# Four image layers on one core: layer 1's buffers placed over those its neighbours release first, with its norm's sums and its attention turns rearranged

## The chip, the cores and the metric

The kernel runs on one core of a Trainium2 chip. A core has a matrix engine (TensorE, called PE; its weight loads are listed apart as PEld), a vector engine (VectorE, DVE), a scalar engine (ScalarE, ACT) and a general one (GpSimd, POOL), and a sequencer that only issues transfers (SyncE, SP). ACT and POOL can issue transfers too, each on a queue of its own. Each engine works through its instructions in order and waits for others by semaphores. The metric is the time of one execution on the device in microseconds (us). Three runs of the kernel before took 5497.55, 5501.04 and 5502.83 us.

## What is computed

Eight images of 56 x 56 points and 192 channels pass four layers. Each layer adds its result to its input, and its input is first normalized over groups of channels (`_gn`). Cut to what matters here:

```python
# layer 0: gated Toeplitz products along rows and columns
p, q, v = silu(x @ p_w.T + p_b), silu(x @ q_w.T + q_b), silu(x @ v_w.T + v_b)
out = (p * (toeplitz_rows(q * v, a1) + toeplitz_cols(q * v, a2))) @ o_w.T + o_b
# layer 1: layer norm over channels, roll by (3, 3), attention in 7 x 7 windows
x = (x - mu) * rsqrt(var + EPS) * gamma + beta
win = roll(x, (-3, -3)) cut into 64 windows of 49 points
attn = softmax(q * scale @ k.T + rel_bias + mask)      # 6 heads of 32
out = roll((attn @ v) @ w_proj + b_proj, (3, 3))
# layer 2: projection to 384 channels, 3 x 3 convolution, four scans, norm, projection back
proj = einsum('bhwd,dc->bhwc', x, W_in) + b_in
local = conv3x3(proj)
mixed = 0.25 * (scan_lr + scan_rl + scan_tb + scan_bt) + local
out = layernorm(mixed) @ W_out + b_out
# layer 3: 7 x 7 convolution, layer norm, two dense layers with gelu
x = x + L0(_gn(x)); x = x + L1(_gn(x)); x = x + L2(_gn(x)); x = x + L3(_gn(x))
```

## The kernel before

The four layers run one after the other, each for all eight images. Between layers the images go through DRAM: layer 0 writes `x1`, layer 1 writes `x2`, the first half of layer 2 writes `pd`. A layer's buffers come from pools that are opened for it and closed after it, so a new pool lies over the memory of an old one. A tile's first write then waits until all that lay there has been read, tile by tile. Layer 0's and layer 1's image buffers stand at the right end of the memory (`raws`, then `l1x` with three buffers), the others at the left, in the order in which they are first asked for.

**Layer 0** ends, for each image, with gates: `layer0_gate` (L475) goes over four pieces of 392 columns and for each projects, applies silu, turns the Toeplitz result and multiplies, and adds the output to the image; `layer0_gate_last` (L539) does so for the last 64 channels. Beside image b+1's products run the store of image b to `x1` and the statistics of image b (`stats`, L610: 12 `bn_stats` on DVE and an aggregate). For the last image these come after everything else (L696 to L699). The Toeplitz results stand in two buffers `os`; the last channels' results share the first of them.

**Layer 1** works on an image in four groups of 16 windows. `layer1_norm` (L775) is a generator: a plan of letters decides when each of its steps is issued. It copies the image, scaled by the group norm, into windows (`windows`, eight copies for a group, into `xr`), squares them on ACT (`squares`), sums channels of the windows and of their squares with matmuls against `ones32` (L844 and L848: for two groups, three channel blocks each, 12 matmul calls), forms the variance (L855, L859), then `rs = (var + eps) ** -0.5` by three small steps (`finish`: DVE, ACT logarithm L820, ACT exponential L822), spreads it over the partitions with a matmul (L827, `rstd`) and multiplies the windows by it on DVE (L832, `scaled`). For image 0 (`first`) the copies are shared by POOL, ACT and DVE, and the sums come for group 0, group 1, and groups 2 and 3.

`layer1_scores` (L873) projects queries and keys (letter Q, L886), values (V, L901) and the scores (E, L916). On DVE the bias and mask are added (L921) and the maximum taken (L923), POOL subtracts it (L924); in the next group ACT takes the exponential (X, L928), DVE sums (L933) and inverts (L934), POOL multiplies (Y, L935). `layer1_mix` (L942) turns the shares with PE transposes (T, L956, three tiles `et_ps` for each half image), copies them out (L961 on ACT, L963 on DVE), multiplies them with the values (P, L971, two tiles `po`), and projects (R, L990 and L997; added to the image by DVE at L1004). PE's results stand in PSUM in rings of buffers: three named "mm" (projections, values, sums, `rstd`, the first half of `pr`, and the third turn), two named "et" (the first and second turn, `po`, the second half of `pr`).

The order in layer 1's main loop is written by hand (L1508): for each group the letters of a plan are issued one by one; N is one step of the norm of the next image, 13 of them in a group. Within the loop, `manual_schedule` keeps PE, ACT, DVE and POOL in this order. Loads of the image after next are issued in groups 1 to 3 (L1521), stores after each group (L1545). Memsets and constants before the loop, and layer 2's first half, are ordered by the scheduler.

**Layer 2, first half** (L1552): `layer2_image` loads an image, `layer2_scale` normalizes it into `xn` in one DVE instruction, `layer2_in` projects it with PE in 15 pieces of 384 columns, adds the bias on DVE into `pt` and stores `pt` to `pd`; for the last image the first 16 channels are stored first. **Layer 2, second half** (`layer2_mix`, L1061): 24 groups of 16 channels, for all images together, are loaded from `pd` (`zc`), with their convolution weights (`wt`), and pass matmuls, copies and DVE scans. The first group's loads are spread over the SP, POOL and ACT queues.

## Time and profile before

| quantity | us |
|---|---|
| median of three runs | 5501.04 |
| the profiled execution | 5505.7 |
| its span, first to last instruction | 5503.9 |
| layer 0, projections (0 to 766) | 766 |
| layer 0, products and gates (766 to 1948) | 1182 |
| PE's pause before layer 1's first sums | 14.4 |
| layer 1, first sums to last matmul (1962.7 to 2945) | 982 |
| PE's pause before layer 2's first matmul | 24.5 |
| layer 2, first half (2969.5 to 3207.8) | 238 |
| PE's pause before layer 2's second half | 24.2 |
| layer 2, second half, mixing (3231.9 to 3850) | 618 |
| layer 2, output (3850 to 4340) | 490 |
| layer 3 (4340 to 5504) | 1164 |

Over the span PE is busy 4998.8 us (91%), DVE 3053.1 (55%), ACT 2311.1 (42%), POOL 1877.9 (34%). How to read what follows: a busy PE is modelled from its instructions' starts and may be a little off; a line in order of time merges neighbours of one kind ("x12"); an engine's idle time is put down to whatever released it last.

### The profile page before, as it was taken

What the parts mean: (1) busy time and instruction counts of PE and PEld (TensorE: products, weight loads), DVE (VectorE), ACT (ScalarE), POOL (GpSimd) and SP (SyncE); (2) the same over time, 40 slices, a digit from 0 to 9 for tenths busy, and PEclk for the clock granted to TensorE, in tenths of its full rate; (3) what the DMA queues carried; (4) which work ended last, traced back from release to release, by engine and by line L of the source; (5) the groups of instructions that cost most, each with busy time, mean ns of one, the idle gap of its engine ahead of it and who ended that gap; (6) DMA issues with size and microseconds to landing.
All of it is one profiled execution on the core that took longest, in us unless ns stands there. A gap on an engine that the chain in (4) does not pass through costs nothing. (4 is left out here: it accounts for less than half of the span.)

```text
span 5503.9 us, 113538 instructions
## 1 busy us (share of the span) xinstructions
PE 4998.8 (91%) x49428; PEld 3379.9 (61%) x49428; DVE 3053.1 (55%) x4273; ACT 2311.1 (42%) x3109; POOL 1877.9 (34%) x1583
## 2 busy tenths in 40 slices
PE   7999969999999979999987989998798787999999
PEld 6778866666666645666665757775344586444444
DVE  4555533555555456666666868888777214343331
ACT  3444435555555434444441025554576302333333
POOL 5555555555555434344431023333011101001000
PEclk9999989999999989999998999999899898999999
DMA  5989896777777623223225757675777696212211
GB/s 148 234 222 232 222 269 261 272 273 275 277 276 272 201 68 85 77 81 86 82 59 156 270 214 235 230 237 188 182 218 220 241 340 235 65 61 87 70 40 27
DMA packets 533335, 1002.87 MB, mean 182 GB/s; under 512 B 256104, under 2 KB 467812, under 8 KB 501460
## 3 DMA queue, kind: packets, MB, share of 16 engines
q1 hardware_dynamic: 519984, 945.58, 53.5%
q0 software_dynamic: 8576, 40.69, 2.3%
q10 hardware_dynamic: 4276, 9.32, 0.6%
q8 instruction: 389, 6.37, 0.5%
q14 instruction: 110, 0.90, 0.1%
HBM read 665.22 MB, written 346.75 MB: 184 GB/s over the span
## 5 line engine op out<-in xcount | busy, mean ns | idle before, releaser
L465 POOL COPY lc<-lt 128x896 f32<-128x896 f32 (+1 forms) x320 | 616.4, 1934 | 513.9 <-PE op L473 490.7
L432 PE MATMUL qv<-w_qv_sb,x 64*112 64x256 f32 (+1 forms) x5376 | 692.0, 410 | 24.0 <-DVE act L438 20.1
L432 PEld LDWEIGHTS qv<-w_qv_sb,x 64*112 64x112 f32 x5376 | 592.5, 176 | 112.5 <-DVE act L438 32.2
L438 DVE TENSOR_TENSOR act<-qv,b_qv 112x640 f32<-112x640 f32 x448 | 318.7, 752 | 325.4 <-PE qv L432 238.5
L442 ACT ACTIVATE act<-act 112x640 f32<-112x640 f32 x448 | 300.3, 683 | 414.3 <-DVE act L438 403.7
L408 POOL TENSOR_TENSOR qv<-act 112x320 f32<-112x320 f32 x448 | 346.5, 799 | 288.9 <-ACT act L442 193.6
L473 PEld LDWEIGHTS op<-rc,lc 128*56 128x56 f32 x9216 | 329.6, 135 | 124.2 <-issue 65.9
L1366 PE MATMUL ph<-y,w_sb 64*128 64x392 f32 x2304 | 398.9, 499 | 6.5 <-ACT hid L1370 6.5
L473 PE MATMUL op<-rc,lc 128*56 128x56 f32 x9216 | 354.5, 221 | 55.1 <-ACT rc L465 38.2
L1377 PE MATMUL po<-hid,w_sb 128*64 128x392 f32 x2304 | 386.3, 494 | 0.0
L1384 DVE TENSOR_TENSOR x<-x,z 128x392 f32<-128x392 f32 x96 | 72.8, 759 | 520.3 <-ACT z L1382 520.3
L1097 PE MATMUL cv<-zc,wt 128*128 128x224 f32 x1536 | 312.8, 355 | 24.9 <-DMA zc<-pd 24.2
L1097 PEld LDWEIGHTS cv<-zc,wt 128*128 128x128 f32 x1536 | 290.3, 189 | 68.3 <-issue 53.1
L1366 PEld LDWEIGHTS ph<-y,w_sb 64*128 64x128 f32 x2304 | 220.7, 189 | 176.5 <-issue 26.5
L506 PE MATMUL y<-pp,w_o_sb 128*64 128x392 f32 x1536 | 309.0, 499 | 5.8 <-DVE pp L500 5.8
L1112 POOL TENSOR_TENSOR rows<-rows,loc 128x896 f32<-128x896 f32 x96 | 223.3, 2326 | 261.9 <-ACT rows L1108 204.6
L483 PE MATMUL pj<-xn,w_p_sb 64*128 64x392 f32 x1536 | 289.1, 509 | 19.7 <-ACT pp L490 18.1
L924 POOL TENSOR_TENSOR e<-e,mx 128x1176 f32<-128x1176 f32 x64 | 140.2, 2190 | 462.6 <-DVE mx L923 398.3
L465 ACT COPY rc<-rt 128x896 f32<-128x896 f32 (+1 forms) x160 | 279.9, 1749 | 40.0 <-DMA rt<-right 40.0
L1377 PEld LDWEIGHTS po<-hid,w_sb 128*64 128x64 f32 x2304 | 162.7, 137 | 213.8 <-issue 213.8
L500 DVE TENSOR_TENSOR pp<-pp,ot 128x784 f32<-128x784 f32 x128 | 124.1, 970 | 292.6 <-PE ot L495 239.9
L1115 DVE TENSOR_TENSOR_SCAN sums<-dec,rows 64x896 f32<-64x896 f32 x96 | 278.5, 2901 | 1.3
(252 smaller groups left out, 9194.8 us busy)
## 6 DMA issues: line engine op xcount, KB each, us to landing
lt<-left SPq DMA_DIRECT2D x72, 1792.0 KB
rt<-right SPq DMA_DIRECT2D x72, 1792.0 KB
left<-qv SPq DMA_DIRECT2D x224, 252.0 KB
right<-qv SPq DMA_DIRECT2D x96, 504.0 KB
wt<-in_band_dram SPq DMA_DIRECT2D x23, 2048.0 KB
zc<-pd SPq DMA_DIRECT2D x187, 232.0 KB
pd<-pt SPq DMA_DIRECT2D x7, 5568.0 KB
bm<-bmask SPq DMA_DIRECT2D x64, 588.0 KB
```

What stands on the lines that cost most here:

```text
L408: nc.gpsimd.tensor_tensor(qv[:, s, s0:s1, k], *(acts[s][:, which, 0:n].rearrange("p (s d) -> p s d", d=64) for which in range(2)), ALU.mult,)
L432: nc.tensor.matmul(ps[s][:, which, 0:n], x[64 * s:64 * s + 64, j, bass.ts(i, 2 * W)], w_qv[64 * s:64 * s + 64, j, which, 64 * s0:64 * s1], ...
L438: nc.vector.tensor_tensor(acts[s][:, :, 0:n], ps[s][:, :, 0:n], b_qv[:, :, 64 * s0:64 * s1], ALU.add)
L442: nc.scalar.activation(acts[s][:, :, 0:n], acts[s][:, :, 0:n], AF.Silu)
L465: copy(c[:, 0:nu], raw.rearrange("p (w u d) -> p u d w", u=nu, d=64 // nu)[:, :, d0:d0 + 8])
L473: nc.tensor.matmul(op[64 * u:64 * u + W, i, :], lc[:, u, i], rc[:, u, i], start=True, stop=True)
L483: nc.tensor.matmul(ps[:, s, 0:TT], w_p[64 * s:64 * s + 64, j, 128 * c:128 * c + 128], xn[64 * s:64 * s + 64, j, bass.ts(t, TT)], start=(j ...
L506: nc.tensor.matmul(y[64 * s:64 * s + 64], w_o[:, 2 * g + u, 64 * j:64 * j + 64], pp[:, u, s], start=(u == 0), stop=(u == 1),)
L1097: nc.tensor.matmul(dst, wt[:, c4 + i, 128 * q:128 * q + 128], zc[:, :, c4 + i, q:q + NPAIR], start=(q == 0), stop=(q == 1),)
L1115: nc.vector.tensor_tensor_scan(_reversed(sums[0:64]), d[0:64], _reversed(rows[0:64]), 0.0, ALU.mult, ALU.add)
L1366: nc.tensor.matmul(ps[:, s, 0:TT], w0[64 * s:64 * s + 64, j, m * 128:(m + 1) * 128], y[64 * s:64 * s + 64, j, ts], start=(j == 0), stop=(j ...
L1377: nc.tensor.matmul(ps[64 * s:64 * s + 64], w1[:, m, 64 * j:64 * j + 64], hid[:, m, s], start=(m == 0), stop=(m == 5),)
```

## The change

Layer 1's pool asks for its buffers in a new order, by hand, so that image 0's windows lie over layer 0's operand copies and its first image buffer, and the weights and the second half's windows over layer 0's output buffers. Image 0's window copies all go to POOL, as do its squares, and are issued behind layer 0's last products instead of behind its last store; its sums come for two groups at a time. The plan's order holds from layer 1's first instruction. Weights are loaded from POOL's queue. Layer 0's last statistics are issued piece by piece during the last gates.

For images 1 to 7, POOL first adds the three channel blocks of the windows and of their squares, and the sums take one matmul call where there were three. Two empty steps stand between the exponential and `scaled`. The steps for image b+2 begin in group 3 of image b (before: those for image b+1 in group 0 of image b). The second tile of each turn moves from ring "et" to ring "mm".

Layer 2's images take the three buffers of layer 1's images; images 0 and 1 are loaded in groups 1 and 2 of layer 1's last image. Image 0 is scaled by ACT in three pieces. The last image is projected in two ranges of channels, 0 to 128 and 128 to 384, each stored when it is done, the second from ACT's queue. In the mixing half the buffers of the two load turns get places of their own, behind the work buffers; the memsets of `dec` come after the first loads, and those loads use the SP and POOL queues.

```diff
@@ layer0_gate, layer0_mix
-            yield
+            yield t
...
-        run(gate)
+        side, ready = stats(nimg - 1, x[-1]), 6
+        for t in gate:
+            ready += 0 if t is None else 3
+            if ready:
+                next(side)
+                ready -= 1
         store(nimg - 1, x[-1])
-        run(stats(nimg - 1, x[-1]))
+        run(side)
@@ layer1_norm
-        xr = pool.tile([128, XR], F32, name="xr")
+        xr = pool.tile([128, XR], F32, name=f"xr{b % 2}", bufs=1)
...
-                if first and n % 3 == 1:
-                    nc.scalar.activation(dst, src, AF.Identity, bias=sh, scale=sc)
-                else:
-                    eng = nc.vector if first and n % 3 == 2 else nc.gpsimd
-                    eng.tensor_scalar(dst, src, sc, sh, ALU.mult, ALU.add)
+                nc.gpsimd.tensor_scalar(dst, src, sc, sh, ALU.mult, ALU.add)
...
+                if first:
+                    nc.gpsimd.tensor_tensor(dst, src, src, ALU.mult)
+                else:
+                    nc.scalar.activation(dst, src, AF.Square)
...
+        if first:
+            sqs = {}
+            for g in (0, 1, 2, 3):
+                run(windows(g))
+                if g < 2:
+                    sqs[g] = square(g)
+                    run(squares(g, sqs[g]))
+                if g == 0:
+                    first()
+            for g0 in (0, 2):
+                if g0:
+                    for g in (2, 3):
+                        sqs[g] = square(g)
+                        run(squares(g, sqs[g]))
+                ps = stat()
...
+                to = variance(ps, g0, 2)
+                run(finish(to))
+                if g0 == 0:
+                    scaled(0)
                     yield
-        if first:
+                scaled(g0 + 1)
+                yield
+            scaled(2)
+            yield
             return
+
+        for g0 in (0, 2):
+            tiles = []
+            for g in (g0, g0 + 1):
+                sq = square(g)
+                xs = pool.tile([128, 4, 2, WN], F32, name="xs", bufs=2)
+                tiles.append((xs, sq))
+                yield from windows(g)
+                nc.gpsimd.tensor_tensor(xs, in_slots(xr, 3 * g * GW), in_slots(xr, (3 * g + 1) * GW), ALU.add)
+                nc.gpsimd.tensor_tensor(xs, xs, in_slots(xr, (3 * g + 2) * GW), ALU.add)
+                yield from squares(g, sq)
+                yield
+                for j in (1, 2):
+                    nc.gpsimd.tensor_tensor(sq[:, :, 0], sq[:, :, 0], sq[:, :, j], ALU.add)
+                yield
+            yield
+            ps = stat()
+            for k, (xs, sq) in enumerate(tiles):
+                nc.tensor.matmul(
+                    ps[32 * k:32 * k + 32, 0:TT], ones32, xs.rearrange("p k z t -> p (k z t)"), start=True, stop=True
+                )
+                nc.tensor.matmul(
+                    halves(ps[64 + 32 * k:96 + 32 * k, 0:TT]), ones32, sq[:, :, 0], start=True, stop=True
+                )
+            variance(ps, g0, 2)
+            yield
         yield from finish(slice(0, 128))
+        yield
+        yield
         for g in range(4):
             scaled(g)
             yield
@@ layer1_mix
-            tag, bufs = ("mm", 3) if i == 2 else ("et", 2)
+            tag, bufs = ("mm", 3) if i else ("et", 2)
@@ layer2_scale
+        if b:
+            tc.keep_in_program_order(nc.vector.tensor_scalar(xn[:, :, :, 0:W], x, sc, sh, ALU.mult, ALU.add))
+        else:
+            for rows in (slice(0, 6), slice(6, 14), slice(14, R2)):
+                nc.scalar.activation(xn[:, :, rows, 0:W], x[:, :, rows], AF.Identity, bias=sh, scale=sc)
@@ layer2_in
-        for i in range(nh):
+        for c0, c1 in ((0, 128), (128, C2)) if b + 1 == nimg else ((0, C2),):
+            for i in range(nh):
...
+            (nc.scalar if c0 else nc.sync).dma_start(pd[b][:, c0:c1], pt[:, c0:c1])
@@ layer2_mix
-            ema = resident("ema", nc.gpsimd, pool)
...
-            nc.gpsimd.memset(dec, 0.36)
-            nc.gpsimd.memset(dec[:, :, 0:1], 0.0)
+            for z, n in (("loc", 6), ("rows", 3), ("sums", 6)):
+                pool.tile([128, 4 * NG], F32, name=z, bufs=n)
+            ema = resident("ema", nc.gpsimd, pool)
...
-                wt = pool.tile([128, CG2, 256], F32, name="wt2")
+                wt = pool.tile([128, CG2, 256], F32, name=f"wt2_{g % 2}", bufs=1)
...
-                n, queues = (CG2, (nc.sync,)) if g else (4, (nc.sync, nc.gpsimd, nc.scalar))
+                n, queues = (CG2, (nc.sync,)) if g else (4, (nc.sync, nc.gpsimd))
-                zc = pool.tile([128, nimg, CG2, P2], F32, name="zc2")
+                zc = pool.tile([128, nimg, CG2, P2], F32, name=f"zc2_{g % 2}", bufs=1)
...
             loaded, now, n = [load(0)], None, C2 // CG2
+            nc.gpsimd.memset(dec, 0.36)
+            nc.gpsimd.memset(dec[:, :, 0:1], 0.0)
@@ layer 1, before and in its loop
+        for name, shape in (("xr0", [128, XR]), ("rs1", [128, TT]), ("msq", [128, TT]), ("sq0", [128, 2, 3, 4 * WN])):
+            kept(shape, name)
...
+        def weights():
+            nc.gpsimd.dma_start(sel, a["sel"])
+            nc.gpsimd.dma_start(wg, wgd)
+            nc.gpsimd.dma_start(w_proj, a["w_proj"])
+
+        own = layer1_norm(0, x[0], pool, psum, consts, weights)
...
-        for _ in range(11):
-            next(own)
+        next(own)
         nc.vector.memset(S, 0.0)
...
-        for kind in "QVQVQEE":
+        for n, kind in enumerate("QVQVQEE"):
             ahead[kind].pop(0)()
-            for _ in range(4):
+            if n == 2:
+                for e in es[0] + es[1]:
+                    nc.gpsimd.memset(e, 0.0)
+            if n >= 2:
                 next(own, None)
...
+        steps = normalize(1)
         for b in range(nimg):
...
+                if g and b + 1 == nimg and g <= nimg and g < 3:
+                    xb.append(layer2_image(g - 1, xpool, nc.sync))
...
                 if g == 3:
                     run(steps)
+                    steps = normalize(b + 2)
@@ layer 2, first half
-        x = [layer2_image(0, xpool, nc.scalar)]
-        w_in = resident("w_in", nc.scalar, pool)
-        b_in = resident("b_in", nc.scalar, pool)
+        x = xb
+        w_in = resident("w_in", nc.gpsimd, pool)
+        b_in = resident("b_in", nc.gpsimd, pool)
...
-            if b + 1 < nimg:
-                x.append(layer2_image(b + 1, xpool, nc.sync))
+            if b + 2 < nimg:
+                x.append(layer2_image(b + 2, xpool, nc.sync))
```

## The prediction

> **What bounds the kernel now.** I read the busy table by stage first. TensorE (PE) works 91% of the span, but not evenly: between two layers it stands still while the next layer's data is laid out. So I read the order of time at the three seams that the diff touches: layer 0 to 1, layer 1 to 2, and layer 2's input to its mixing.
>
> ```profile
> 1944.10 4.16 PE L506 MATMUL y<-pp,w_o_sb 128*64 128x392 f32 x22 [0.26 <-DVE pp L500]
> 1948.38 0.72 POOL L782 MEMSET xr<- 128x720 f32 x1 [45.30 <-issue]
> 1962.71 1.52 PE L844 MATMUL stat<-xr,ones 128*32 128x392 f32 x2 [14.44 <-POOL xr L805]
> 1974.10 4.29 PE L886 MATMUL qk_ps<-xr,wg 64*128 64x392 f32 x12 [1.73 <-DVE xr L832]
> 2015.92 1.53 PE L956 MATMUL et_ps<-ident,e 128*128 128x128 f32 x12 [0.22 <-POOL e L935]
> ...
> 2966.23 2.90 DVE L1030 TENSOR_SCALAR xn<-x,scsh 128x5040 f32<-128x5040 f32 x1 [18.44 <-DMA x<-x]
> 2969.48 6.77 PE L1044 MATMUL pin<-w_in_sb,xn 64*128 64x384 f32 x28 [24.53 <-POOL xn L1031]
> ...
> 3208.65 0.32 SPq L1058 DMA_DIRECT2D pd<-pt  x1
> 3231.94 13.36 PE L1097 MATMUL cv<-zc,wt 128*128 128x224 f32 x57 [24.19 <-DMA zc<-pd]
> ```
>
> Columns: start, duration (us), engine, line, operation; in brackets the idle time before it and what ended it. Seam 1: PE ends layer 0 at 1948.3, the first projection of layer 1 (L886) starts at 1974.1, the first turn (L956) at 2015.9; GpSimd (POOL) idled 45.3 us beforehand because its target memory was taken. Seam 2: 24.5 us for the last store, a load and a 2.9 us scaling. Seam 3: 24.2 us for the last image's way to DRAM and back.
>
> Then layer 1's steady state, by windows from first turn to first turn of groups 0, 1, 2, 3 of image 1, and one group of the last image, which normalizes nothing; then PE's waits in this layer:
>
> ```profile
> 2136.40:2163.80 27.40, 26.84 (x564) 17.59 (x564) 18.36 (x32) 13.82 (x24) 16.28 (x21) 1.00 0.39 110
> 2163.80:2196.10 32.30, 28.16 (x567) 17.81 (x566) 21.15 (x36) 15.88 (x28) 16.14 (x19) 0.99 0.39 98
> 2196.10:2227.80 31.70, 29.38 (x548) 19.73 (x547) 21.89 (x36) 10.20 (x17) 7.80 (x4) 0.91 0.21 59
> 2227.80:2255.30 27.50, 24.22 (x542) 16.88 (x541) 18.96 (x33) 11.28 (x20) 10.48 (x9) 1.00 0.24 69
> 2879.85:2906.30 26.45, 24.16 (x542) 16.88 (x541) 18.00 (x31) 10.98 (x19) 8.75 (x4) 1.00 0.25 71
> ...
> PE po L971 <- DVE et L963: 16.0, 29, 1.5
> PE rstd L827 <- ACT rs L822: 15.3, 7, 2.2
> PE et_ps L956 <- POOL e L935: 6.0, 6, 1.0
> ```
>
> After the stage's length come busy time and count of PE, its weight load, DVE, ACT, POOL, then clock and DMA. PE fills 24 to 29 us of each group, DVE 18 to 22, POOL 8 to 16. An image takes 118.9 us (mean of six, 118.2) against 4 x 26.45 = 105.8 bare: normalizing costs 13 us of PE's order. A second limit lies just behind: from the end of a group's first scores to the next turn there are DVE, POOL, ACT, DVE and POOL steps in a row, 11.8 us in the last group (2920.4 to 2932.2), against 12.4 us of PE work there.
>
> **Seam 1.** The new xr0 lies over layer 0's operand copies and image buffer, free at 1902. POOL then makes all four groups: 32 copies at the L805 means of 0.42 to 0.52 (15.4 us), 0.8 of memsets, three DMA issues (1.7), four squares of 588 columns. No POOL row shows a square of that size; 112x320 took 0.87 and 128x1176 took 2.19, and I take 1.15 (4.6 in all). Weights lie over the first output buffer, read until 1916.7, so POOL blocks there for some 7 us and is done near 1933, 15 us before PE needs it. The 2.4 MB of image 0 are issued at 1898 as before; pieces from POOL's queue landed in 6 to 9.5 us, so they feed it. At 1948.3 PE does the sums (12 calls took 2.15 at 1995), then 0.54 ACT, 0.57 and 0.35 DVE, 2 x 0.53 ACT, 0.9 PE, 1.57 DVE, with 0.7 of gaps: first projection at 1956.2, 17.9 earlier. The four memsets of e (1.46 each) wait for layer 0's last buffers, end near 1950, and the other four squares near 1955, before the second sums ask for them (about 1969). The interleaved bn_stats (0.48 each) fit the 1.1 to 6 us holes of DVE in the gates. From there to the first turn: projections and values 14.8 us by their rows, the second sums with the same chain unhidden and 1.7 of scaling about 8, scores 0.9, then 11.8; 35.6 against 41.8. **Seam 1: -24** (-14 if the second part gives nothing, -30 if the chain hides).
>
> **Steady state.** (a) Sums: POOL first adds the three channel blocks, so PE does 4 calls for 12, 1.3 us less per pair, 2.6 per image. POOL gains 16 adds of 128x392 per image; between 0.73 (112x256) and 2.19 (128x1176), I take 0.85. (b) Two empty steps stand between the exponential (L822) and L827: the 2.2 us wait per image goes, and PE isn't cooled by it (clock 0.91 in that window, transposes at 2.3 to 2.8 instead of 1.53 after it). (c) The turn's second tile moves from the two "et" buffers to "mm", so the mix's second buffer no longer waits for DVE's copy of it: the two mixes of a group lose about 0.4 each. (d) Steps for image b+2 start in group 3 of image b, 52 slots for 45 steps. Cost: POOL work queued between its subtraction L924 and L935, which the turn waits for. The old trace shows the price: 1.9 us put there (memsets and two copies at 2251.2) gave 1.0 of PE wait. Now 2.5 lands there in groups 3 to 0 and 0 to 1, 1.9 in 2 to 3: 1.7, 1.7 and 1.0 lost. By group: 13.3 (14.1 - 0.8, turn to scores) plus the larger of 12.4 and 11.8 + delay, plus sums 0.7 and rstd 0.9 each: 26.8, 27.6, 28.3, 29.0 = 111.7, that is -6.5 for each of six images, -39. Image 0's own groups: -6 (its four scalings now come in one lump, costing about 5 of that gain). Image 7: 4 x 0.8 = -3. **Steady: -48** (-22 with adds at 2.0; -65 if no delay shows).
>
> [...]
>
> **Seam 2.** Images 0 and 1 of layer 2 load in groups 1 and 2 of image 7 into buffers whose stores are 30 us or more old (POOL 0.74 each, inside slack; on SP two issues of 0.6 each stand ahead of the scores' mask loads, which were issued 10 us and more ahead of use). Scaling of image 0 goes to ACT in three pieces; at L1370's 914 ns per 784 columns the first (1008) takes 1.2 after ACT's last copy at 2940.9. Weights go by POOL's queue after its last L935 at 2935.0 and, by POOL landings of 4 to 15 us, are there at 2939 to 2950. PE's last matmul ends at 2944.95. **-26**: 24.5 less 0.7, plus 2.2 for a start at full clock (28 passes took 6.8 instead of 4.5); -15 with a late weight.
>
> **Seam 3.** The last image goes in 128 and 256 columns. 128-column passes aren't in the trace; the bounds are a third of today's 1.94 per row pair (0.65) and twelve times 0.0925 from 64x192 passes (1.11); with 1.3 to 1.35 for the rest that is 0 to +8; I take **+5**. The first 1.9 MB leave 20 us before PE ends, so the loads run under the second part. Their memory is image 6's pt, whose 5.6 MB store needs 17 us at 325 GB/s (234 GB/s at share 0.72); the loads then land about when PE ends. The store of the second part goes by ACT's queue, where only mixing copies stand behind it, and so doesn't block SP's loads; the last image's load waits on POOL's queue, with 3.4 us of dec memsets behind it, which the first scan wants 10 us after PE's start. I leave 4 of the 24.6 us: **-20.6** (0 if pt frees late). The next group's buffers lie over the last pt: 3.7 MB out and 3.9 MB in at 380 GB/s end 26 us after PE, wanted at 22.6: **+3** (0 to 8).
>
> **Sum.** -24 - 48 - 26 + 5 - 20.6 + 3 = -110.6 on the profiled execution's 5505.7 (span 5503.9): 5395. The median of the runs, 5501.0, is 4.7 lower: **5390**.
>
> **Rivals.** *Seams only:* POOL's adds eat the steady gain. For it: 0.5 us of slack on that chain. Against: 8 to 16 busy us in 27. Price: -62.6, 5438. *Third seam only moves:* the loads share DMA with 5.6 MB of stores and all mixing buffers lie under old ones. For it: DMA share 1.03 at 3210 to 3240. Against: the range before is at 0.72. Then -24 - 48 - 26 + 8: 5411. *Slower:* the turns take 17 instead of 15 places per group in the ring of three "mm" buffers, so the third tile waits for ACT's copy of the projection before it (0.59, with 0.84 of moving beside it on ACT's queue). The rest is worth -85 without (c); at over 1.3 us per turn, 64 turns, it decides; at 1.55 it gives 5515. Against: ACT starts that copy before the projection has ended, and PE's waits for such buffers total 10 us now. *Not what it says:* a tile's memory isn't free when I think and seams 1 and 2 stay; then -43 or so, 5458.
>
> **Chances.** Forecast 0.63 (own range 5355 to 5420), third seam moving 0.12, seams only 0.10, seams staying 0.05, slower 0.08, no change 0.02. Range 5352 to 5450: it leaves out the slower and equal cases, half of the staying seams and the tails. Faster by over 0.2% (11 us, about what a measurement can tell from no change) 0.90, same 0.02, slower 0.08.
>
> **What would show it.** L886 first at about 1956; first turn near 1992; turn-to-turn sums near 112; no PE wait on rs L822 and hardly any on et L963; L1044 within 2 us of layer 1's last matmul; L1097 within 6 us of the last pin. I'm wrong if PE waits on POOL's L935 by more than 2 us per group, or on "mm" readers, or if the loads of the first mixing group still end a wait of 15 us or more.

## The result, and the profile after

The changed kernel takes 5456.15 us (median of six, 5454.42 to 5466.29) against 5501.48 for the kernel before in the same comparison (5497.55 to 5509.90). The ratio is 0.9921, 95% interval 0.9908 to 0.9933: faster by 45, where 110 were forecast, and 6 outside the upper end of the forecast range. The profiled execution took 5463.48, its span is 5461.7.

The two profiled spans, cut at the same events (us; the forecast is the prediction's term):

| from, to | before | after | difference | forecast |
|---|---|---|---|---|
| start, last matmul of layer 0 | 1948.3 | 1937.4 | -10.9 | 0 |
| to layer 1's first turn | 67.6 | 47.4 | -20.2 | -24 |
| to the first turn of its last group | 916.3 | 962.6 | **+46.3** | **-48** |
| to layer 2's first matmul | 37.3 | 13.6 | -23.7 | -23.8 |
| to the first matmul of the mixing | 262.5 | 238.9 | -23.6 | -17.8 |
| to the end | 2272.0 | 2261.9 | -10.1 | +3 |

The forecast -26 of seam 2 is split here: 2.2 of it (a start at full clock: 1.00 was granted in the first 6.75 us, before 0.70 in the first 6.72) lies in the row below. The first row was not forecast and isn't explained: in nineteen profiles of kernels with after's layer 0 the first sums of layer 1 start between 1933.9 and 1949.9, all but one of them before 1948, but of the kernel before there is a single profile. In the last row the second mixing group's wait costs 9 by the third group's start, but the 21 groups from there take 24.3 each where they took 24.9, 12 less in all, and from the last `cv` to the last `mx` it is 8 less (21.2, then 13.3). What made these shorter is not known. Seam 1 gave 4 less than forecast, the other two as much or more; one stage ended 94 from its forecast, the wrong way. Without the first and the last row the gain would be about half.

The order of time of after, PE, at the three seams:

```profile
1937.34 0.52 PE L870 MATMUL stat<-xr,ones 128*32 128x392 f32 x1
...
1943.30 1.67 PE L830 MATMUL rstd<-rs,sel 32*128 32x392 f32 x2 [3.77 <-ACT rs L825]
1946.69 4.29 PE L934 MATMUL qk_ps<-xr,wg 64*128 64x392 f32 x12 [1.73 <-DVE xr L835]
...
1984.79 1.53 PE L1004 MATMUL et_ps<-ident,e 128*128 128x128 f32 x12
...
2960.95 14.46 PE L1097 MATMUL pin<-w_in_sb,xn 64*128 64x384 f32 x88
...
3199.81 3.34 PE L1145 MATMUL cv<-zc,wt 128*128 128x224 f32 x16 [0.70 <-DVE pt L1105]
...
3225.94 6.27 PE L1145 MATMUL cv<-zc,wt 128*128 128x224 f32 x16 [9.38 <-DMA zc<-pd]
```

The sums now follow layer 0's last matmul without a pause (14.4 before), layer 2's first matmul has no bracket at all (24.5 before), and the mixing starts 0.70 after the last projection (24.2 before). The last line is what is left: the second mixing group waits 9.38, and its first matmuls then run at about half speed (6.27 for 16 at a granted clock of 0.50, later 3.24 at 1.00).

Image 1 by windows from first turn to first turn, as the prediction showed it for the kernel before:

```profile
2116.21:2145.30 29.09, 24.97 (x549) 16.98 (x548) 21.11 (x36) 13.68 (x23) 17.37 (x19) 1.00 0.38 106
2145.30:2174.60 29.30, 26.74 (x552) 18.48 (x552) 18.20 (x31) 12.80 (x24) 15.47 (x14) 0.94 0.42 106
2174.60:2210.30 35.70, 30.66 (x546) 20.69 (x544) 24.36 (x40) 11.20 (x19) 10.45 (x9) 0.86 0.18 53
2210.30:2242.00 31.70, 26.64 (x540) 17.52 (x540) 17.16 (x30) 12.80 (x22) 23.06 (x26) 0.95 0.21 59
```

The sum is 125.8 (forecast 111.7, before 118.9). PE's own work did shrink: 24.97 in the first group, where 26.84 stood before. But the third and fourth groups are 4 us longer each, PE's clock is below 1 in three of four, and POOL is busy 23 of 31.7 in the last. The waits of layer 1's middle (2150 to 2850):

```profile
ACT sq L817 <- POOL xr L806: 72.7, 16, 11.4
...
PE v_ps L949 <- DVE x L1052: 22.4, 22, 2.3
PE et_ps L1004 <- POOL e L983: 16.8, 10, 2.4
PE po L1019 <- DVE et L1011: 15.1, 7, 2.5
PE qk_ps L934 <- ACT qk L938: 10.6, 5, 2.1
```

The first line was not there before: ACT stands 72.7 us at its squares; the longest of these waits, once an image, is 11.4. The prediction gave waits in ACT's queue no term. Here is that longest wait, ACT, then POOL, then PE, in order of time:

```profile
2221.80 0.84 ACT L941 COPY k<-qk 64x784 f32<-64x784 f32 x1 [0.17 <-DVE qk L939]
2234.00 0.70 ACT L817 ACTIVATE sq<-xr 128x588 f32<-128x588 f32 x1 [11.36 <-POOL xr L806]
2234.61 1.19 ACT L976 ACTIVATE e<-e 128x1176 f32<-128x1176 f32 x1
2235.70 0.56 ACT L938 ACTIVATE qk<-qk_ps,bq 128x392 f32<-128x392 f32 x1
```

```profile
2219.58 1.10 POOL L806 TENSOR_SCALAR xr<-x,scsh 128x196 f32<-128x196 f32 x2
2226.68 2.19 POOL L972 TENSOR_TENSOR e<-e,mx 128x1176 f32<-128x1176 f32 x1 [6.00 <-DVE mx L971]
2228.85 2.18 POOL L806 TENSOR_SCALAR xr<-x,scsh 128x196 f32<-128x196 f32 x4
2230.99 2.18 POOL L972 TENSOR_TENSOR e<-e,mx 128x1176 f32<-128x1176 f32 x1
2233.16 0.81 POOL L806 TENSOR_SCALAR xr<-x,scsh 128x84 f32<-128x84 f32 x2
```

```profile
2231.99 2.21 PE L949 MATMUL v_ps<-wg,xr 64*128 64x192 f32 x22 [0.40 <-DVE qk L939]
2236.32 0.92 PE L934 MATMUL qk_ps<-xr,wg 64*128 64x392 f32 x2 [2.11 <-ACT qk L938]
2238.27 3.84 PE L934 MATMUL qk_ps<-xr,wg 64*128 64x392 f32 x10 [1.03 <-ACT v L954]
```

Read backwards: PE's projection waits 2.11 for a PSUM buffer that ACT's copy L938 must empty; L938 stands behind the square L817; the square waits for the last of its group's window copies on POOL (L806, ended 2233.97); those stand behind the subtraction L972, which itself waited 6.00 for DVE's maximum of the same group's scores. The exponential L976, whose input was ready at 2228.9, ran at 2234.61. So work for the *next* image, whose sums PE does 12 us later and whose first scaling some 65 us later, closes a ring through four queues around *this* image's softmax.

### The profile page after: what moved, and what is told of

The parts are those of the page before. It is cut to its first block, busy times and chain, and to the rows that moved or that the text cites. A ratio compares the mean times of both kernels' runs of the same rounds, so it can differ in the third digit from the quotient of the medians.

```text
span 5461.7 us, 113572 instructions
## 1 busy us (share of the span) xinstructions
PE 4977.1 (91%) x49378; PEld 3402.4 (62%) x49378; DVE 2982.5 (55%) x4274; ACT 2308.7 (42%) x3088; POOL 1991.8 (36%) x1732
## 3 DMA queue, kind: packets, MB, share of 16 engines
q1 hardware_dynamic: 520400, 944.42, 53.8%
## 4 chain that ended last, share of the span: by engine, by line
PE 71%; DVE 10%; ACT 6%; POOL 5%; DMA 5%; issue 3%; SPq 1%; ACTq 0%; DVEq 0%; POOLq 0%
PE qv L432 9%; PE po L1428 7%; PE ph L1417 7%; PE cv L1145 5%; PE mx L1172 5%; PE pj L483 5%; PE y L506 4%; PE pin L1097 4%; PE op L473 3%; PE po L1242 3%; PE qk_ps L934 3%; PE cps L1320 3%; DVE ln_st L200 2%; PE ot L495 2%; PE v_ps L949 2%
## 5 line engine op out<-in xcount | busy, mean ns | idle before, releaser
L1145 PEld LDWEIGHTS cv<-zc,wt 128*128 128x128 f32 x1536 | 290.8, 190 | 53.8 <-issue 45.1
L1160 POOL TENSOR_TENSOR rows<-rows,loc 128x896 f32<-128x896 f32 x96 | 203.0, 2115 | 327.0 <-ACT rows L1156 233.5
L465 ACT COPY rc<-rt 128x896 f32<-128x896 f32 (+1 forms) x160 | 279.8, 1749 | 24.4 <-DMA rt<-right 24.4
L1344 POOL TENSOR_TENSOR yl<-yl,dwb 128x1344 f32<-128x1344 f32 (+1 forms) x40 | 86.0, 2174 | 548.5 <-DMA yl<-yd 548.5
L972 POOL TENSOR_TENSOR e<-e,mx 128x1176 f32<-128x1176 f32 x64 | 140.1, 2189 | 397.0 <-DVE mx L971 385.1
```

The lines of the kernel that those rows point to most:

```text
L465: copy(c[:, 0:nu], raw.rearrange("p (w u d) -> p u d w", u=nu, d=64 // nu)[:, :, d0:d0 + 8])
L1145: nc.tensor.matmul(dst, wt[:, c4 + i, 128 * q:128 * q + 128], zc[:, :, c4 + i, q:q + NPAIR], start=(q == 0), stop=(q == 1),)
```

## The experiments

The first theory, formed from the lines above: the steady state loses because (A1) the squares stand directly behind their own group's copies and (A2) the scalings stand ahead of the third group's turn. Rivals: the turn's buffer from the mm ring (B), POOL's adds (C). Ratios are to the kernel before on the same chip; 0.001 is 5.5 us.

| kernel | us | ratio, 95% interval |
|---|---|---|
| changed kernel | 5456.15 | 0.9921 [0.9908, 0.9933] |
| e1_seams | 5422.81 | 0.9856 [0.9841, 0.9871] |
| e2_turn_back | 5472.64 | 0.9950 [0.9935, 0.9965] |
| e3_sums_back | 5413.97 | 0.9843 [0.9827, 0.9860] |
| e5_squares_late | 5428.25 | 0.9880 [0.9854, 0.9906] |
| e6_scale_late | 5472.99 | 0.9941 [0.9923, 0.9959] |
| e7_sums_back_scale_late | 5425.60 | 0.9854 [0.9840, 0.9869] |
| e8_seams_turn | 5403.87 | 0.9818 [0.9795, 0.9840] |
| e9_adds_off | 5457.86 | 0.9915 [0.9899, 0.9932] |
| e10_spread | 5377.75 | 0.9783 [0.9766, 0.9799] |
| e11_spread_queues | 5396.50 | 0.9824 [0.9810, 0.9839] |
| e12_sums_back_scale2 | 5408.07 | 0.9841 [0.9827, 0.9856] |
| e13_start | 5416.20 | 0.9854 [0.9835, 0.9874] |
| e14_empties | 5383.22 | 0.9793 [0.9779, 0.9806] |
| e15_spread_adds | 5435.87 | 0.9887 [0.9874, 0.9901] |
| e16_seams_turn_again | 5398.81 | 0.9826 [0.9806, 0.9846] |
| e17_spread_adds_spaced | 5451.20 | 0.9920 [0.9906, 0.9933] |
| e18_spread_squares_early | 5414.39 | 0.9850 [0.9837, 0.9864] |
| e19_spread_later | 5379.20 | 0.9787 [0.9774, 0.9800] |

### The seams alone, and the turn

`e1_seams`: the changed kernel, with images 1 to 7 normalized as before (sums, squares, start, no empty steps) and the second tile of a turn in "et".

```diff
-        for g0 in (0, 2):
-            tiles = []
...
+            for g in (g0, g0 + 1):
+                yield from windows(g)
+            for g in (g0, g0 + 1):
+                sqs.append(square(g))
+                yield from squares(g, sqs[-1])
...
-            tag, bufs = ("mm", 3) if i else ("et", 2)
+            tag, bufs = ("mm", 3) if i == 2 else ("et", 2)
...
-        steps = normalize(1)
         for b in range(nimg):
...
+            steps = normalize(b + 1)
```

> Everything of the change except the work on images 1 to 7 inside layer 1: there the statistics go back to twelve matmuls on windows and squares, the two empty steps go, the turn's second tile goes back to the et ring, and the normalization of the next image starts with the image again, not one group earlier. Theory A (the seams gained what they were forecast to, and the steady state, forecast at -48, lost some 37 between the first turns of images 1 and 7): the time falls by about 37 to 48, to 5408 to 5420, with 118 us from first turn to first turn as before. Rival (the seams moved the loss in, the steady state is slow because of the new memory layout or the transfers, not because of its own edits): about 5456, with 124 us an image kept.

It took 5422.8, 33 less than the whole change, and images 1 to 6 take 118.5 us on the mean, as before (118.2). So the seams bring 79 by themselves, and the steady-state work as a whole gives back some 36 (0.0065). The memory layout is not to blame.

`e2_turn_back` undoes only the line with `tag` in the changed kernel; `e8_seams_turn` (run again as `e16_seams_turn_again`) adds only that line to e1.

> Only the turn's second tile goes back from the mm ring to the et ring. Theory A (the loss is in the engines' in-order queues: ACT's squares standing behind POOL's window copies, the scalings standing ahead of the turn on DVE): the turn is at best a side matter, 0 to +10, so 5452 to 5466. Rival B (the third buffer taken from the mm ring is what holds the projections): faster by 15 or more, under 5441. The prediction's term (-0.4 us a mix, 64 mixes) would give +25, 5481.

> The seams with one part of the steady-state work more: the turn's second tile in the mm ring; old sums, old start, no empty steps. If the turn is worth what taking it out of the changed kernel showed (+16), 5422.8 falls to about 5407. If the earlier start and the two empty steps are what makes the kernel with the sums back (5414) faster than the seams alone, it stays at 5420 to 5425. The prediction's term for the turn (-0.4 a mix) would give 5398.

> The kernel of the seams and the turn again, as the common base of the next two runs, on one chip with them: 5404 (ratio 0.982).

Without it 5472.6, 16 worse; with it 5403.9 and 5398.8, 21 and 16 better than e1 by the ratios. Rival B falls: the third "mm" buffer is a gain of 16 to 21 wherever it stands. In the changed kernel PE's waits for the mm ring in a turn (`et_ps` on ACT's copy of v) total 1.6 us in 700, while the mix's wait on DVE's copy of the turn grows from 15.1 to 25.9 without the edit.

### The squares' place and the adds

`e5_squares_late` keeps POOL's adds and changes the order inside the 18 steps; `e3_sums_back` takes the adds out and puts both groups' copies first; `e9_adds_off` takes only the adds out. Both have e1's twelve matmuls.

```diff
@@ e5_squares_late
             yield from windows(g0)
             xs_adds(g0, tiles[0][0])
             yield
+            sqs = squares(g0, tiles[0][1])
+            for n, _ in enumerate(windows(g0 + 1)):
+                if n >= 2:
+                    next(sqs)
+                yield
@@ e9_adds_off
                 yield from windows(g)
-                nc.gpsimd.tensor_tensor(xs, in_slots(xr, 3 * g * GW), in_slots(xr, (3 * g + 1) * GW), ALU.add)
-                nc.gpsimd.tensor_tensor(xs, xs, in_slots(xr, (3 * g + 2) * GW), ALU.add)
                 yield from squares(g, sqs[-1])
                 yield
-                for j in (1, 2):
-                    nc.gpsimd.tensor_tensor(sq[:, :, 0], sq[:, :, 0], sq[:, :, j], ALU.add)
                 yield
```

> The adds on POOL and the four matmuls are kept; only the order of the steps inside each 18-step pair changes: a group's squares on ACT come three or more steps behind the window copies they read, with the other group's copies or adds between. Theory A (ACT's queue stands at a square until POOL has made its copies): ACT's wait on POOL's copies (72.7 us between 2150 and 2850) falls below 20, g3 to g0 falls from 31.7 to 27 or 28, and the time by 20 to 35, to 5421 to 5436. Rival B (mm ring) or C (POOL's adds): within 8 of 5456.

> Only the sums for images 1 to 7 go back: no adds on POOL, both groups' windows first, then both groups' squares, then twelve matmuls; five empty steps per pair keep the statistics, the finish and the scalings at the same steps of the plan. Theory A: the eight extra matmul calls cost 2.6 an image more (+16 over six images), the squares stand four steps behind the copies they read for the first group and so ACT's wait on POOL falls: net -10 to -25, 5431 to 5446. Rival C (the sixteen adds make POOL late for the shares' multiply and nothing else): also faster, by the 2.4 us that the turn waits on POOL at g0 to g1, about -15, but with ACT's wait on POOL's copies unchanged near 70 us. The prediction's own step (the sums as sums gain): +16, 5472.

> The changed kernel with only the adds on POOL gone: twelve matmuls in place of four, the squares still directly behind their group's windows, every step at its old slot. With the three others this makes a table of two (adds or matmuls; squares early or late: 5456, 5428, here, 5414). Theory A with two causes that add up: the adds cost 14 more than the matmuls they save, the squares' place 28, so 5442. If the squares stand only because the adds fill POOL ahead of the copies, then the squares' place is worth little without adds: about 5414 to 5424.

| | adds on POOL, 4 matmuls | 12 matmuls |
|---|---|---|
| squares directly behind their copies | 0.9921 (after) | 0.9915 (e9) |
| squares some steps behind | 0.9880 (e5) | 0.9843 (e3) |

The squares' place costs 0.0041 to 0.0072 (23 to 40 us), without adds more than with them, so the adds aren't what makes it cost. In e5 the waits of PE's projections for ACT's copies, 15.7 in after (`qk_ps` on ACT's copies of qk and v), fall to 2.3. ACT's wait on POOL's copies is 71.3 in e9 and is gone from the lists of e5 and e3; the fourth group's step, 31.6 in after and in e9, is 26.1 in e5 and 24.8 in e3 (means of five images). The expectation for e9 that two causes add up (5442) missed by 16: with early squares the adds cost nothing, perhaps because ACT is late anyway. With late squares they cost 0.0037, 20 us, where a gain of 16 to 18 was forecast.

These kernels also differ in other steps. `e18_spread_squares_early` changes nothing else, in the fastest kernel:

```diff
             for g in (g0, g0 + 1):
-                yield from windows(g)
-            for g in (g0, g0 + 1):
                 sqs.append(square(g))
+                yield from windows(g)
                 yield from squares(g, sqs[-1])
```

> The fastest kernel (scalings spread, 5378, ratio 0.978) with one thing changed: a group's two squares on ACT are issued directly behind that group's window copies, as in the changed kernel, not behind both groups' copies. No adds, the same number of steps, the same instructions. Theory A (ACT's queue stands at the square until POOL has made the copies; behind it stand the exponential and the copies of projections): slower by 25 to 45, 5403 to 5423, with ACT's wait of the squares on POOL's copies back at some 70 us between 2150 and 2850 (none in the kernel it is made from). Rival (the squares' place only matters together with the adds on POOL): within 8 of 5378.

5414.4 against 5377.8, +37. From the list of waits (2150 to 2850) of e18, where e10 has none of these lines:

```profile
ACT sq L821 <- POOL xr L810: 92.4, 21, 7.1
...
PE stat L902 <- POOL xr L810: 10.6, 11, 1.1
...
PE stat L906 <- ACT sq L821: 5.3, 11, 0.5
```

Same instructions, same number of steps: that the squares' place costs is shown, and the rival (only together with the adds) falls. But the 37 are not all paid through ACT's queue. In this kernel no empty step stands behind the squares, so most of the price is direct: the sums wait 0.9 for POOL's copies and 0.5 for the squares, twice an image, 2.8 of the 4.7 us that an image loses (117.6 for 112.9 on the mean of images 1 to 6). The values' projection waits 0.4 for ACT's copies, twice an image (4.8 in the 700 us, 0.4 in e10). For the ring in the changed kernel, where empty steps keep the sums from waiting, e5 is the closer measure.

`e15_spread_adds` and `e17_spread_adds_spaced` put the adds into the fastest kernel, without and with two empty steps between the last add and the sums.

> The fastest kernel so far (scalings spread, 5378, ratio 0.978) with the sums by POOL's adds and four matmuls, the squares three or more steps behind the copies they read. The prediction's step (2.6 an image less for the matrix engine): 5360. Theory A (the adds stand on POOL between its subtraction and the shares' multiply, which the turn waits for; in the pair of kernels with late squares they cost 14 to 20): slower by 8 to 20, 5386 to 5398.

> The fastest kernel with POOL's adds and four matmuls per pair as in e15_spread_adds, but with two empty steps between the last add and the sums. In e15 the sums waited 3.3 us twice an image for POOL's last add, 46 us over seven images, of the 58 that it lost. If that wait was all, the rest is 5378 + 12 = 5390, or a gain if the adds are worth what the prediction said (5360). If the adds cost by filling POOL ahead of the shares' multiply as well, 5395 to 5415.

Both are far worse, +58 and +73, and neither settles the adds' price. In e15 the sums waited 3.2 and 3.3 us in two groups of an image for the last add. In e17 that wait is 0.5, in one group, but its extra steps push the first scaling to the last slot of the third group, and the projections of the next wait 4.2 for it; PE waits 32.4 us for POOL's multiply (2150 to 2850), against 4.9 in e10. In every kernel that had both forms, the adds were no gain; that POOL, busy 23 of 29 us in e17's first group, is late with the shares' multiply is seen in its waits, but not separated by a run from the shift of the scalings.

### The empty steps, the start, and PE's clock

Each added alone to the kernel of the seams and the turn:

```diff
@@ e14_empties
         yield from finish(slice(0, 128))
+        yield
+        yield
         for g in range(4):
@@ e13_start
+        steps = normalize(1)
         for b in range(nimg):
-            steps = normalize(b + 1)
...
                     run(steps)
+                    steps = normalize(b + 2)
```

> The base with the two empty steps between the exponential and the scalings, nothing else: the scalings move from the fourth to seventh slot of the third group to the sixth to ninth. The prediction's step: the matrix engine's wait on ACT's rs (2.2) goes, -2.2 an image less 1.0 for the later scalings: -8 in all, 5396. Theory A (the wait goes, but the four scalings then meet the second turn and the projections and cost as much): within 5 of the base.

> The base with the steps of the next image begun one group earlier, nothing else: the sums fall into the fourth and first group, the finish and the four scalings into the second. Theory A (what counts is how many scalings stand in one group, not which group): the base's time within 8, 117 us an image. Rival (the earlier start is itself a loss, as the kernel with the sums back suggests, some 10): slower by 10 or more. The prediction's step counted it as part of a gain of 6.5 an image.

The empty steps gain 16 (0.0033; 8 expected, and theory A's 0 missed), the earlier start loses 17 (0.0028; theory A's "no matter which group" missed). The order of time of e16, PE, shows why two steps are worth so much:

```profile
2505.33 2.65 PE L927 MATMUL qk_ps<-xr,wg 64*128 64x392 f32 x11
2510.16 0.92 PE L830 MATMUL rstd<-rs,sel 32*128 32x392 f32 x2 [2.19 <-ACT rs L825]
2511.02 1.91 PE L997 MATMUL et_ps<-ident,e 128*128 128x128 f32 x12
2512.86 2.02 PE L1012 MATMUL po<-et,v 49*32 49x49 f32 x96
2514.81 1.67 PE L830 MATMUL rstd<-rs,sel 32*128 32x392 f32 x2
2516.41 4.21 PE L942 MATMUL v_ps<-wg,xr 64*128 64x192 f32 x24
2520.55 2.30 PE L830 MATMUL rstd<-rs,sel 32*128 32x392 f32 x4
2522.78 2.82 PE L997 MATMUL et_ps<-ident,e 128*128 128x128 f32 x12
```

PE pauses 2.19 for the exponential of the finish. Some two us later everything takes up to twice as long for about 14: 24 value matmuls 4.21 (2.22 elsewhere), a turn 2.82 (1.53). The group from 2511.02 has a granted clock of 0.79 and lasts 33.0; where the same group of another image keeps 1.00 it lasts 28.9. The two groups around the scalings in e16 (the second group of image 2, then the third of image 4, with clock 0.79), then in e14 (both of image 1):

```profile
2251.19:2282.58 31.39, 27.51 (x567) 18.51 (x566) 21.30 (x36) 15.85 (x28) 15.72 (x19) 1.00 0.39 101
2511.02:2544.05 33.03, 32.22 (x547) 22.32 (x547) 21.80 (x36) 10.19 (x17) 8.14 (x4) 0.79 0.20 57
```

```profile
2143.21:2171.28 28.07, 26.76 (x565) 17.47 (x565) 19.04 (x34) 14.49 (x26) 15.10 (x18) 1.00 0.45 112
2171.28:2201.76 30.48, 27.25 (x549) 17.89 (x549) 23.58 (x39) 11.35 (x19) 8.75 (x4) 1.00 0.21 61
```

With the empty steps the wait is gone and the clock of the third group stays at 1.00 in images 0 to 6. Over images 1 to 5 the second group falls from 31.3 to 28.4; the third stays (30.7 and 30.5), because the later scalings cost 1.6 there (30.5 for 28.9 at clock 1.00) and the half speed had cost 1.8 on the mean. In e13 the pause is the same 2.19, but the group after it has 0.77 to 0.86 in all five images from 1 to 5; in e16 it varies between 0.79 and 1.00. Why the lower clock followed the shifted pause in all five isn't settled. The padded form of e3, which holds both parts, is 0.0021 above the mean of e8 and e16, and the two alone sum to -0.0005; the intervals (some 0.003 on either) allow both.

### The scalings

`e6_scale_late` puts six more empty steps ahead of the scalings in the changed kernel, `e7_sums_back_scale_late` six and `e12_sums_back_scale2` two in e3.

> The changed kernel with six more empty steps between the finish and the scalings: the four scalings (a matmul into the mm ring and two DVE multiplies of 1.57 us each) move from the third to sixth slot of the third group, around its turn, to the ninth to twelfth slot, behind its turn and mix and among its projections. Theory A (a scaling placed ahead of the turn holds DVE and an mm buffer that the turn's copies need): g2 to g3 falls from 35.7 to 31 to 33, the wait of the turn on DVE's scaling (0.62) and of the mix on DVE's copy of the turn (2.5) go, and the time falls by 15 to 30, to 5426 to 5441. Rival (the scalings cost DVE the same wherever they stand, since the projections' adds need DVE too): within 8 of 5456.

> The kernel with the sums back (twelve matmuls, no adds on POOL, squares behind both groups' windows, 5414) and the scalings six steps later as in the run of that name. Theory A: the two are independent, g2 to g3 falls from 33.3 to 30 to 31 and the time to 5394 to 5404. Rival as there: 5414.

> The kernel with the sums back (5414) with the scalings two slots later, fifth to eighth of the third group, all behind its first three turns. Theory A as mended by the two runs with the scalings six later (there the cost only moved, from the mix's wait on DVE's copy to the projections' wait on the scaled windows): between, 5410 to 5420, since what costs is four scalings in one group, not the slot. Rival (it is the turn that they stand ahead of): 5400 or below.

A2 falls: +11 by the ratios (the intervals overlap a little), +6 and nothing. The wait only changed its place: in the third group the mix's wait on DVE's copy (2.5 an image in after) went, and the projections waited 3.1 on the scaled windows in e6, 3.4 in e7. That left another reading, four scalings (two DVE multiplies of 1.57 each) in one group. `e10_spread` takes e8, puts one empty step behind the finish and gives each group one scaling; `e19_spread_later` moves them one slot on.

```diff
         yield from finish(slice(0, 128))
-        for g in range(4):
-            scaled(g)
-            yield
+        yield
+        scaled(0)
+        shared[b] = scaled
+        yield
...
+                late = (b + 1, 1) if g == 3 else (b, g + 2)
+                slots = 0
                 for kind in plan:
                     if kind == "N":
                         next(steps, None)
+                        slots += 1
+                        if slots == 5 and g != 2 and late[0] in shared:
+                            shared[late[0]](late[1])
```

> The kernel of the seams and the turn (old sums, old start, second tile in the mm ring; 5403.9) with the four scalings of an image spread, one to a group, at the fifth slot (behind the first mix): the first in the third group after one empty step, the others in the three groups that follow, each still ahead of the projections that read its group. Theory A (the groups that carry stat and scalings take 31.6 and 31.9, those without 26.9, because four scalings of 3.1 us of DVE and one wait on the finish stand in one group): the third group's wait on ACT's rs (2.2) goes, three groups' worth of DVE work find gaps, and an image falls from 117.3 to 112 to 114, the time to 5370 to 5385. Rival (DVE has no gaps: each scaling costs its 3 us wherever it stands): 117 an image, 5400 to 5408.

> The fastest kernel with the scalings one slot later (sixth, behind the values' projection) and a second empty step ahead of the first, to see whether it can be bettered: 5368 to 5380. If the sixth slot is worse (the scaling then stands right ahead of the second turn's copies on DVE): 5385 to 5400.

5377.75, the lowest of all: 0.9783, faster than the changed kernel by 78 and than the one before by 117. Image 1 by windows:

```profile
2104.00:2131.70 27.70, 27.52 (x567) 18.03 (x567) 19.88 (x34) 13.87 (x24) 16.26 (x21) 1.00 0.39 108
2131.70:2162.30 30.60, 29.29 (x568) 19.24 (x567) 20.61 (x36) 14.43 (x26) 15.06 (x18) 0.94 0.40 104
2162.30:2188.90 26.60, 24.78 (x543) 17.02 (x543) 19.55 (x33) 11.36 (x19) 8.75 (x4) 1.00 0.25 70
2188.90:2216.70 27.80, 24.95 (x544) 17.18 (x544) 20.56 (x35) 11.33 (x20) 10.53 (x9) 1.00 0.23 68
```

DVE's load is even (19.6 to 20.6; after: 17.2 to 24.4), PE waits under 3 us in any group of images 1 to 6, and these take 112.5 to 114.5, close to the steady state that was forecast for the change, reached with other means. One slot later makes no difference.

But e10 differs from e8 in two things: the scalings are spread, and the wait on `rs` is gone. `e14_empties` takes away the wait alone, with the four scalings still in one group. It has 0.9793, with an interval that overlaps e10's, and its images 1 to 6 take 113.0 on the mean, where e10's take 112.9. So the spread as such is not shown to bring anything; the 0.0039 between e8 and e10 can be the wait and the clock behind it.

### The second mixing group's loads

`e11_spread_queues` is e10 with those loads on two queues.

```diff
-                n, queues = (CG2, (nc.sync,)) if g else (4, (nc.sync, nc.gpsimd))
+                n, queues = (CG2, (nc.sync, nc.gpsimd)[:1 + (g == 1)]) if g else (4, (nc.sync, nc.gpsimd))
```

> The same, and the loads of the second mixing group go over two queues, SP's and POOL's, in place of SP's alone. The steady state as in the run before it; the matrix engine's wait for the second group's zc (9.4 in the changed kernel) falls by about 4, half of the 8.0 us that SP takes to issue the eight, so 4 less from the first pin matmul to the end. If the wait is set by the load of wt alone, which starts when the last store of pt has landed, nothing changes there.

Slower by 0.0041, 23 us. POOL's order of time, then PE's:

```profile
3133.59 0.54 POOL L1132 DMA_DIRECT2D zc<-pd  x1 [9.85 <-DMA pd<-pt]
3134.12 0.35 POOL L1186 MEMSET dec<- 128x128 f32 x1
3134.30 1.60 POOL L1132 DMA_DIRECT2D zc<-pd  x3
3135.91 6.13 POOL L1158 TENSOR_TENSOR rows<-rows,loc 128x896 f32<-128x896 f32 x3
```

```profile
3146.01 1.83 PE L1170 MATMUL mx<-sums,ema_sb 128*112 128x448 f32 x2 [11.18 <-DVE sums L1161]
```

The load's target lies under the last `pt`, so its issue waits 9.85 for that store; POOL's adds for the first group stand behind it, DVE's scans behind those, and PE waits 11.18 for the scans. It is the squares' mistake again on another engine. But it only takes the place of e10's wait of 9.7 for `zc`: at the third group's start both kernels are level (53.8 and 53.6 from the first `cv`), and up to the seventh. The loss comes behind that (12 up to the last `cv`, 8 from there to the last `mx`, by the starts in both traces), and its cause is not known; whether the load of `wt` alone sets the 9.4 stays open.

## Why the prediction was wrong, point by point

**Seam 1 (-24, measured -20.2).** Right in kind. POOL blocked 5.7 at the weights (7 guessed), its squares took 1.15 as taken. From the first sums to the first projection it took 9.35, not 7.9: the chain to `rs` alone held PE 3.77. From there to the first turn 38.1, not 35.6.

**Seam 2 (-26).** Right: layer 2's first matmul follows layer 1's last without a gap.

**Split and seam 3 (+5, -20.6, +3).** The first half of layer 2 takes 238.2, as before (238.3), so the split cost no more than the 2.2 that its start at full clock was to save, where 5 were given. The first group waits 0.70, where 4 were left (of a pause of 24.2; the sum had 24.6). The second group's wait was undersized: 9.38 and a start at half speed (6.27 for 3.24), where 3 (0 to 8) was given. By the third group that had cost 9. Even so the row to the end is 13 better than its forecast, by later groups and an end that got shorter for a reason not known: the good total there is luck.

**Steady state (-48, measured +46).** The step that failed is the sum by groups, "the larger of 12.4 and 11.8 + delay". It followed one chain (POOL's subtraction, exponential, multiply, turn) and priced what is put on POOL's queue ahead of L935; it had no term for what is put on ACT's queue. The diff moves each group's squares directly behind that group's copies, an edit that the prediction costed at nothing without naming a cover. It costs 37 where it is the only difference (e18, there mostly as sums that wait for it), 23 to 40 in the table of two by two. The start one group earlier, the second thing that the sum had no price for, costs 15 to 17 (e13), and the adds, forecast as a gain, bring none.

Of its parts: (a) the eight matmul calls saved are seen (PE 24.97 for 26.84 in the first group) and bring no time; an add takes 0.95 to 1.03, not 0.85, and PE waits 2.4 for POOL's multiply at the end of the first group, over the limit of 2 that the prediction set itself. (b) is right and undersized: 16 to 18, where the wait less a later scaling gives 8 (so expected for e14); the missing half is the clock behind the pause, by the groups of e16 and e14 above, which the prediction saw (0.91, transposes at 2.3 to 2.8) and priced only through its group formula. (c) is right: 16 to 21 for 25.6. (d), taken as room for 45 steps, costs 15 to 17 alone. From e1 to after, by ratios: turn -0.0034, start with empty steps and padding +0.0021, squares +0.0072, adds +0.0006, together +0.0065.

**The signs it named.** First projection at 1946.7 and first turn at 1984.8 came earlier than 1956 and 1992, with layer 0 itself 10.9 earlier. No wait on `rs` in the loop: right. "Hardly any" on `et`: wrong, 15.1 in 700 us. Waits on readers of the "mm" buffers, a sign of being wrong, did come (10.6 and 22.4 in the list above, 5.1 on ACT's copy of v), but not from the turn's tile: with it put back (e2) they are 10.5, 23.1 and 5.1. Turn-to-turn sums of 112: wrong, 124 to 127 in five images of six.

**Rivals.** "Seams only" named the right direction and its price (5438) is near the seams' run (5423), but the loss went beyond eating the gain, and the squares were the larger part of it, not the adds that it named. "Slower by the mm ring" is refuted. "Not what it says" gave 5458, close to the measured time, by luck: its reason did not occur, since every seam opened, and its price was mis-added. With seams 1 and 2 gone the terms leave -48 + 5 - 20.6 + 3 = -60.6, so 5440; -43 leaves out the third seam too.

## What to carry to other kernels

Before placing work for later into an engine's queue, ask what that work itself waits for, and what urgent work stands behind it: here a square, issued right behind the copies it reads, held the softmax of the current image or, with no empty steps behind it, its own sums: 23 to 40 us in this kernel's variants. In these runs slack work did best several steps behind its producer. And a stall of PE is to be priced with what the clock did after such stalls in the trace (4 us more behind 2.19 in the image of e16 shown), not by its length alone.

## What the runs showed of the hardware

A pause of 2.19 us in PE was followed, in the image of e16 shown, after about two us of full speed by some 14 us at half speed (4.21 for 2.22, 2.82 for 1.53), so a wait of 2 cost 4 more (33.0 for 28.9). It varies between images of one run: behind the seven such pauses of e16 the half speed lasted from nothing to 14 us (granted clock 1.00 to 0.79 in the same group).
